# Seven products of quarters for half of an output product, in the middle of a fused attention and FFN block

## The chip, the cores and the metric

The kernel runs on one core of a Trainium2 chip. The core has five engines with queues of their own: TensorE (PE) multiplies matrices into PSUM, VectorE (DVE), ScalarE (ACT) and GpSimd (POOL) work on SBUF (and the first two on PSUM), and SyncE (SP) only issues transfers. ACT and POOL issue transfers too. Each engine takes its instructions strictly in the order of its queue. The metric is device time in microseconds (us), the median of some runs; a profiled execution gives the trace.

## The reference

Four batches of 1024 tokens with 512 channels go through an attention block and a linear FFN, both with a layer norm that is scaled and shifted per batch, and a gate:

```python
h = _layernorm(x) * (1 + ca) + sa
x = x + ga * attention(h)        # qf = h Wq^T, kf = h Wk^T; scores = 16 heads' equal q k^T
h = _layernorm(x) * (1 + cb) + sb
x = x + gb * (h @ sum_of_8_factors / sqrt(8) + bias)
```

All 16 heads have the same scores, since each head's factor is one; so the probabilities are one 1024 x 1024 matrix a batch, and V and the output projection can be folded into one matrix. Everything is float32.

## The kernel before

**The algebra.** With Wvo = Wv^T Wo^T made once, attention is softmax(q k^T) · n · W: n is the normalized x, W (`make_w`) is Wvo with the batch's scale and gate. The kernel forms Z^T = n^T · P^T first, for half of the tokens at a time (`z_steps(b, half)`), then Z · W (`attn_out`, one tile of 128 tokens at a time), divides by the softmax's denominator and adds to x. A constant row c1 is added to x (`add_c1`). Then comes the second layer norm (`ln2(b, g)`, half g), whose transposed result goes through the FFN (`ffn`, `make_f`).

**Z by quarters.** Both Z products already use Strassen's scheme: seven products m1 to m7 of quarters in place of eight, in the order m1, m5, m2, m6, m7, m3, m4 for batches 1 to 3. Their sums are taken ahead: `n_sums` on POOL (s1 to s4, L685 to L694), `p_sums` (L706, L709) and t2, t4 (L743, L779) on DVE. Each product leaves PSUM through ACT (L741, L750) or DVE (L753, L755, L761, L770, L782). L766 and L767 on POOL add two results.

**The output product.** Batches 0 to 2 use `attn_out` for all eight tiles: 4 matmuls (8 records; a float32 matmul has two) of 512 columns at L951, then L956 on DVE takes the product from PSUM, scales it by 1/denominator and adds x, and `stats` follows (L404, L406). Batch 3 uses `attn_out_quarters` for both halves: `quarter_products` makes four sums of Z (L855 to L858), `t_sums` four of W (L842 to L845), seven products of 256 columns run at L870, and DVE combines them into c (L900 to L907; ACT copies the first, L896); then L888 scales c and adds x.

**The scores.** `softmax(b, p)` does one pair of token tiles: scores on PE (L584) into one of two large PSUM tiles, maxima on DVE (L601), exponentials on ACT (L609), a reciprocal (L614), a 32 x 32 block transpose on DVE (L624), and `move_blocks` (L492): 16 transfers issued by SP, which complete the transpose. Pair 3 is done apart (`scores`, `transpose_probs`).

**Order.** While the second Z product of batch b runs (the loop over z1's seven steps k), `places` puts the projections (`project`, L538, with L552 on DVE) and the first three pairs of batch b+1 between its steps. Then come the eight `attn_out` tiles, with pair 3 and `ln2(b, 0)` in between, then the first step of batch b+1's first Z product, `ln2(b, 1)`, and in the next turn of the loop over b the rest of that Z product with `make_f`, the FFN of batch b (L1020, L1025), the bias adds (L1012) and the layer norm and transpose (`ln1`: L404, L416; `hT_by_dma`: L503) of batch b+2.

The order written in the code is a priority, not the order run: before the launch a planner fills each engine's queue by its own estimates of costs, and takes at each point the first-written instruction that it takes to be ready. `tc.keep_in_program_order` pins an instruction behind the one written before it for that engine (the c1 adds L478 have it); `follow(op, others)` pins op behind the others. Both order the queue and wait for nothing.

**Buffers.** `ps_m` has four PSUM buffers for all products. `stg` has four staging buffers (s1, s2, s4, t of one batch), `stp` two ("st": staging of transposes), `prp` two ("pr": probabilities, and c). W and f share one buffer. `ln2` of half 0 issues its 16 transfers on ACT, half 1 on SP; ACT then scales and shifts what has landed (L1002). In the sequence of the FFN, the four tiles of half 0 follow m6 of the next batch's first Z product, and half 1 follows m7.

Of the kernel before, what the change touches and what calls it, by code (L numbers as in the profile page):

```python
# [10 lines left out]
F32 = mybir.dt.float32  # L11
# [19 lines left out]
def kernel(  # L31
# [19 lines left out]
    P = 128  # L51
# [382 lines left out]
    def halves(g):  # L434
        return list(range(g * GT, (g + 1) * GT))
# [34 lines left out]
            load_xa(b + g, 1 - g)  # L470

    bc_c1, bc_ga = {}, {}

    def add_c1(b, tiles):
        if b not in bc_c1:
# [3 lines left out]

            tc.keep_in_program_order(add)  # L480

    def move_blocks(src, dst, *queues, c_outer=False):

        queues = queues or (nc.sync,)
        for i in range(NQ * NQ):
            r, c = divmod(i, NQ)
            if c_outer:  # L490
                r, c = c, r
            queues[i % len(queues)].dma_start(out=dst[ts(c, Q), r], in_=src[ts(r, Q), c])  # L492

    def hT_by_dma(b, g, *queues):

# [78 lines left out]
    def scores(b, p, later=False):  # L574


        qT, kT = qkT[b]
        if p == 0:
            rinv[b] = small.tile([P, NT], F32, tag="ri", bufs=2, name=f"ri_{b}")
        pss = []  # L580
        for i in (2 * p, 2 * p + 1):
            ps = ps_s.tile([P, T], F32, tag="sc", name=f"ps_sc_{b}_{i}")
            for h in range(2):
                nc.tensor.matmul(  # L584
                    ps[:, ts(h, 512)], qT[h * R : (h + 1) * R, ts(i, P)],
                    kT[h * R : (h + 1) * R, :], start=True, stop=True,
                )
            pss.append((i, ps))
        den = small.tile([P, 2], F32, tag="den", name=f"den_{b}_{p}")
        pr2 = prp.tile([P, 2 * T], F32, tag="pr", name=f"pr_{b}_{p}")  # L590


        if by_dma(b, 2 * p // GT):
            view = pr2.rearrange("p (c j k e) -> p k j c e", c=NQ, k=2, e=Q)
        else:
            view = pr2.rearrange("p (k j) -> p k j", k=2)
        probs[b, p] = pr2, view
        maxima = []
        for i, ps in pss:
            nm = small.tile([P, 1], F32, tag="nm", name=f"nm_{b}_{i}")  # L600
            nc.vector.tensor_reduce(nm, ps, AX.X, ALU.max, negate=True)  # L601
            maxima.append(nm)

        def numerators():
            for k, (i, ps) in enumerate(pss):
                pr = view[:, k]
                if len(pr.shape) > 2:
                    ps = ps.rearrange("p (j c e) -> p j c e", c=NQ, e=Q)
                exp = nc.scalar.activation(  # L609
                    pr, ps, AF.Exp, bias=maxima[k], scale=1.0, accum_out=den[:, k : k + 1]  # L610
                )
                if later:
                    tc.keep_in_program_order(exp)
            nc.vector.reciprocal(rinv[b][:, 2 * p : 2 * p + 2], den)  # L614

        if later:
            return numerators
        numerators()
# [171 lines left out]
    def make_w(b):  # L790
        bc = bc_ga[b] if b in bc_ga else spread("ga", b)
        if b + 1 < B:
            w = wbp.tile([P, KC, D], F32, tag="w", name=f"w_{b}")
        else:

            both = ptp.tile([P, 2, KC, D], F32, tag="pt", name=f"w_{b}")
            w, tsum["w"] = both[:, 0], sums_of(both[:, 1])
        for kc in range(KC):
            scaled = nc.vector.scalar_tensor_tensor(
                w[:, kc, :], wvo[:, kc, :], first["ca1"][:, kc, b : b + 1], bc, ALU.mult, ALU.mult  # L800
# [2 lines left out]

                tc.keep_in_program_order(scaled)
        wb[b] = w
        if b + 1 == B:
            t_sums(w, tsum["w"])

    def make_f(b):
        bc = spread("gb", b)  # L810
# [9 lines left out]
        fb[b] = f  # L820
        if b + 1 == B:
            t_sums(f, tsum["f"])

# [20 lines left out]
        tt(t3, b22, b12, ALU.subtract)  # L844
        tt(t4, b21, t2, ALU.subtract)  # L845

    def quarter_products(name, a, m, tm, engine):
# [4 lines left out]
        pr = prp.tile([P, KC, D], F32, tag="pr", name=f"sums_{name}")  # L852
        s1, s2, s3, s4 = sums_of(pr)
        tt = engine.tensor_tensor
        tt(s1, a21, a22, ALU.add)  # L855
        tt(s2, s1, a11, ALU.subtract)
# [19 lines left out]
        return product  # L876

    def attn_out_quarters(b, half):
        product = quarter_products(f"o_{b}_{half}", ZT[b, half], wb[b], tsum["w"], nc.vector)
        c = prp.tile([P, GT, D], F32, tag="pr", name=f"c_{b}_{half}")  # L880

        def cq(i, h):
# [82 lines left out]
    def ln2(b, g, ahead=None, between=None):  # L965
# [99 lines left out]
    for b in range(B):  # L1065
# [148 lines left out]
```

## Time and profile before

| | us |
|---|---|
| median of 3 runs | 518.86 (516.21 to 518.98) |
| profiled execution | 516.97 |
| its span, first to last instruction | 515.2 |
| PE busy (matmuls) | 507.4, 98% |
| DVE busy | 403.8, 78% |
| ACT busy | 91.6, 18% |
| POOL busy | 181.1, 35% |
| granted PE clock, mean | 0.999 |

PE's records are pipelined and overlap, so a record's duration (381 ns for 256 columns, 593 for 512) is longer than the distance between two. Durations of DVE overlap a little too: sums of 128 x 512 elements last 0.68 us by the record and follow each other every 0.60 us.

### The profile page before, as it was taken

Reading aid. Unit: us, or ns where it says so; the run is one execution under the profiler, and the core shown is the slowest. Engines: PE = TensorE matmul, PEld = TensorE weight load, DVE = VectorE, ACT = ScalarE, POOL = GpSimd, SP = SyncE. Lnnn points to the kernel's source line nnn. Section 1 sums busy time; section 2 is a strip of 40 time slices with the busy share of each in tenths; the row PEclk is TensorE's granted clock in tenths of the full one; section 3 lists DMA queues with packets and bytes.
Section 4 is the critical chain, followed back from the end, with each engine's and each line's share of the span. In section 5 each row is a group of like instructions: output and inputs, shape, how many; then the busy total and the mean of one; then the engine's idle time right before and its main releaser. Section 6 shows DMA issues by size and latency. Waiting matters only on the chain.

```text
span 515.2 us, 5746 instructions
## 1 busy us (share of the span) xinstructions
PE 507.4 (98%) x1888; PEld 327.5 (64%) x1888; DVE 403.8 (78%) x638; ACT 91.6 (18%) x148; POOL 181.1 (35%) x183
## 2 busy tenths in 40 slices
PE   9999999999999999999999999999999999999996
PEld 5534787664466547765457457666448488878585
DVE  4759999686999994379999994268999739889895
ACT  1327300231103200222103100122202020002020
POOL 1072324799860453630001344431001040022532
PEclk9999999999999999999999999999999999999999
DMA  8982576378654769114453657304445432003053
GB/s 311 381 309 65 136 169 194 110 241 277 184 137 109 228 199 268 38 27 102 120 135 91 182 143 254 94 0 98 117 106 129 132 107 69 0 1 102 20 174 113
DMA packets 40133, 73.06 MB, mean 142 GB/s; under 512 B 9908, under 2 KB 12468, under 8 KB 40104
## 3 DMA queue, kind: packets, MB, share of 16 engines
q1 hardware_dynamic: 27464, 40.14, 27.5%
q0 software_dynamic: 8416, 27.43, 17.0%
q10 hardware_dynamic: 4224, 5.12, 3.8%
q8 instruction: 15, 0.25, 0.2%
q14 instruction: 14, 0.11, 0.1%
HBM read 34.88 MB, written 8.42 MB: 84 GB/s over the span
## 4 chain that ended last, share of the span: by engine, by line
PE 64%; DVE 15%; SPq 6%; DMA 5%; POOL 3%; issue 3%; ACT 2%; ACTq 1%; DVEq 0%; POOLq 0%
PE ps_z_m L728 24%; PE ps_f L1020 15%; SPq L492 6%; PE ps_o L951 5%; PE ps_f_m L870 5%; PE ps_o_m L870 5%; PE ps_qk L538 4%; DMA pt<-pr 4%; PE ps_wvo L211 3%; DVE pr L624 3%; DVE nm L601 2%; ACT pr L609 1%; DVE hT_f L995 1%; ACTq L492 1%; DVE hT_f L416 1%
## 5 line engine op out<-in xcount | busy, mean ns | idle before, releaser
L728 PE MATMUL ps_z_m<-pt,xn_a 128*128 128x256 f32 x512 | 116.1, 381 | 0.4 <-DVE zt L753 0.4
L728 PEld LDWEIGHTS ps_z_m<-pt,xn_a 128*128 128x128 f32 x512 | 96.4, 190 | 22.2 <-issue 4.9
L1020 PE MATMUL ps_f<-f,hT_f 128*128 128x512 f32 x192 | 83.9, 593 | 0.4 <-ACT hT_f L1002 0.3
L951 PE MATMUL ps_o<-w,zt 128*128 128x512 f32 x192 | 83.7, 594 | 0.0
L951 PEld LDWEIGHTS ps_o<-w,zt 128*128 128x128 f32 x192 | 36.2, 190 | 45.5 <-issue 42.3
L1020 PEld LDWEIGHTS ps_f<-f,hT_f 128*128 128x128 f32 x192 | 36.3, 190 | 44.1 <-issue 39.2
L728 PE MATMUL ps_z_m<-pt,s 128*128 128x256 f32 x256 | 58.2, 380 | 0.0
L728 PEld LDWEIGHTS ps_z_m<-pt,s 128*128 128x128 f32 x256 | 48.4, 190 | 10.9 <-issue 4.7
L609 ACT ACTIVATE pr<-ps_sc,nm 128x1024 f32<-128x1024 f32 x32 | 35.5, 1113 | 88.6 <-DVE nm L601 62.0
L601 DVE TENSOR_REDUCE nm<-ps_sc 128x1 f32<-128x1024 f32 x32 | 37.6, 1210 | 3.8 <-PE ps_sc L584 3.8
L584 PE MATMUL ps_sc<-kT,qT 64*128 64x512 f32 x128 | 34.7, 622 | 1.4 <-ACT pr L609 1.4
L1002 ACT ACTIVATE hT_f<-st_f,mod_sb,mod_cb 128x512 f32<-128x512 f32 x32 | 23.4, 802 | 65.5 <-DMA st_f<-hT_f 41.8
L379 POOL TENSOR_TENSOR fsum<-fsum,factor 128x1024 f32<-128x1024 f32 x14 | 33.7, 2428 | 2.4 <-DMA factor<-in_factors_dram 2.3
L624 DVE STREAM_TRANSPOSE pr<-pr 128x2048 f32<-128x2048 f32 x14 | 32.2, 2297 | 0.5 <-issue 0.2
L741 ACT COPY zt<-ps_z_m 128x512 f32<-128x512 f32 x8 | 4.7, 587 | 153.3 <-PE ps_z_m L728 85.1
L1027 POOL DMA_DIRECT2D out_dram<-x x24 | 13.4, 560 | 49.5 <-DVE x L1025 38.4
L397 POOL TENSOR_TENSOR r_f<-v_f,mhalf 128x4 f32<-128x4 f32 x8 | 12.1, 1516 | 51.3 <-DVE v_f L391 51.2
L728 PE MATMUL ps_z_m<-t,s 128*128 128x256 f32 x128 | 29.0, 380 | 0.0
L538 PE MATMUL ps_qk<-hT_a,wqk 128*128 128x512 f32 x64 | 28.7, 593 | 0.0
L728 PEld LDWEIGHTS ps_z_m<-t,s 128*128 128x128 f32 x128 | 24.2, 190 | 5.4 <-issue 2.3
L397 POOL TENSOR_TENSOR r_a<-v_a,mhalf 128x4 f32<-128x4 f32 x8 | 10.0, 1245 | 46.5 <-DVE v_a L391 46.4
L766 POOL TENSOR_TENSOR zt<-zt 128x512 f32<-128x512 f32 x6 | 7.7, 1283 | 47.2 <-DVE mv L406 27.6
(175 smaller groups left out, 683.4 us busy)
## 6 DMA issues: line engine op xcount, KB each, us to landing
pt<-pr SPq DMA_DIRECT2D x216, 64.0 KB, 2.0
factor<-in_factors_dram POOLq DMA_DIRECT2D x7, 1024.0 KB, 6.6
out_dram<-x POOLq DMA_DIRECT2D x24, 256.0 KB, 3.0
xa<-in_x_dram POOLq DMA_DIRECT2D x20, 256.0 KB, 4.3
x<-in_x_dram POOLq DMA_DIRECT2D x20, 256.0 KB, 6.0
hT_a<-st_a SPq DMA_DIRECT2D x72, 64.0 KB, 3.7
st_f<-hT_f SPq DMA_DIRECT2D x64, 64.0 KB, 2.0
st_f<-hT_f ACTq DMA_DIRECT2D x58, 64.0 KB, 2.1
```

Source lines behind the costliest of these rows:

```text
L379: add = nc.gpsimd.tensor_tensor(part, part, f[r][:, ts(k, 2), :], ALU.add)
L492: queues[i % len(queues)].dma_start(out=dst[ts(c, Q), r], in_=src[ts(r, Q), c])
L538: nc.tensor.matmul(ps[: 2 * R, :], wqkb[b][:, kc, :], hT[:, kc] if b == 0 else hT[:, :, kc], start=(kc == 0), stop=(kc == KC - 1),)
L584: nc.tensor.matmul(ps[:, ts(h, 512)], qT[h * R : (h + 1) * R, ts(i, P)], kT[h * R : (h + 1) * R, :], start=True, stop=True,)
L601: nc.vector.tensor_reduce(nm, ps, AX.X, ALU.max, negate=True)
L609: exp = nc.scalar.activation(pr, ps, AF.Exp, bias=maxima[k], scale=1.0, accum_out=den[:, k : k + 1])
L624: nc.vector.transpose(pr2, pr2)
L728: nc.tensor.matmul(ps[:, ts(dc, 2 * P)], a[:, j, ts(dc, P)], q, start=(j == 0), stop=(j == GT - 1),)
L870: nc.tensor.matmul(ps[:, ts(i, 2 * P)], st[:, kc, ts(i, P)], mv[:, kc, :], start=(kc == 0), stop=(kc == 1),)
L951: nc.tensor.matmul(ps, ZT[b, half][:, kc, ts(j, P)], wb[b][:, kc, :], start=(kc == 0), stop=(kc == KC - 1),)
L1002: nc.scalar.activation(dst, src, AF.Identity, bias=sb, scale=cb1)
L1020: nc.tensor.matmul(ps, hT2[b, g][:, kc, ts(j, P)], fb[b][:, kc, :], start=(kc == 0), stop=(kc == KC - 1),)
```

## The change

In batches 1 and 2 (the second and third) the output product of half 0 is made by `attn_out_quarters`, as in batch 3. It stands in the loop over the second Z product, behind step 3 (m6) and ahead of the first pair of scores; the third pair moves from step 5 to step 6. `make_w` makes the four sums of W for these batches, in a tile of `stp`; the four sums of Z are put into the staging tiles s1 and t of the Z product, so they keep these from the next batch's sums until the products have read them. The c1 adds of half 0 move to step 2, those of half 1 to step 4. After the loop only tiles 4 to 7 are left for `attn_out`; pair 3 of the scores stands after tile 5, and `p_sums` ahead of tile 6. `ln2` of half 0 of batches 1 and 2 pins its transfers on ACT behind the last exponential.

```diff
-    def move_blocks(src, dst, *queues, c_outer=False):
+    def move_blocks(src, dst, *queues, c_outer=False, behind=()):
...
-            queues[i % len(queues)].dma_start(out=dst[ts(c, Q), r], in_=src[ts(r, Q), c])
+            dma = queues[i % len(queues)].dma_start(
+                out=dst[ts(c, Q), r], in_=src[ts(r, Q), c]
+            )
+            follow(dma, behind)
...
+                last_exp[:] = [exp]
...
             w = wbp.tile([P, KC, D], F32, tag="w", name=f"w_{b}")
+            if b > 0:
+                tsum["w", b] = sums_of(stp.tile([P, KC, D], F32, tag="st", name=f"w_sums_{b}"))
...
-        if b + 1 == B:
-            t_sums(w, tsum["w"])
+        if b > 0:
+            t_sums(w, tsum["w", b])
...
-        product = quarter_products(f"o_{b}_{half}", ZT[b, half], wb[b], tsum["w"], nc.vector)
+        sums = None
+        if b + 1 < B:
+
+            n1, t1 = nsum[b][0], nsum[b][4].rearrange("p r j w -> p (r j w)")
+            sums = [n1[:, ts(i, 2)] for i in range(2)]
+            sums += [
+                t1[:, ts(i, 512)].rearrange("p (k d) -> p k d", k=2) for i in range(2)
+            ]
+        product = quarter_products(
+            f"o_{b}_{half}", ZT[b, half], wb[b], tsum["w", b], nc.vector, sums
+        )
...
-        move_blocks(xn.rearrange("p (c n) -> p c n", c=NQ), st, *queues, c_outer=last)
+        move_blocks(
+            xn.rearrange("p (c n) -> p c n", c=NQ), st, *queues, c_outer=last,
+
+            behind=last_exp if g == 0 and 0 < b and not last else (),
+        )
...
-            places = (1 if b == 0 else 0, 2, 3, 4, 5)
+            places = (1, 2, 3, 4, 5) if b == 0 else (0, 2, 3, 4, 6)
...
             step()
+            if b > 0 and k == 3 and nb is not None:
+                attn_out_quarters(b, 0)
             if k in todo:
                 todo[k]()
...
-            if b > 0 and k >= 3 and nb is not None:
-                add_c1(b, range(2 * (k - 3), 2 * (k - 2)))
-            if nb is None and k == 2:
-                add_c1(b, range(NT))
+            if b > 0 and k == 2:
+                add_c1(b, halves(0) if nb is not None else range(NT))
+            if b > 0 and k == 4 and nb is not None:
+                add_c1(b, halves(1))
...
-        for t in halves(0):
+        for t in halves(0) if b == 0 else halves(1)[:2]:
             attn_out(b, t)
-            if t == 2:
+            if t % GT == (2 if b == 0 else 1):
                 scores(nb, 3)
...
-        for t in halves(1)[:2]:
-            attn_out(b, t)
-        if b > 0:
+        if b == 0:
+            for t in halves(1)[:2]:
+                attn_out(b, t)
+        else:
             p_sums(nb, 0)
```

More of the change, by code (lines that the diff above doesn't have):

```diff
@@ L472 @@
     bc_c1, bc_ga = {}, {}
+    last_exp = []
     def add_c1(b, tiles):
@@ L793, in make_w @@
             w = wbp.tile([P, KC, D], F32, tag="w", name=f"w_{b}")
+            if b > 0:
+                tsum["w", b] = sums_of(stp.tile([P, KC, D], F32, tag="st", name=f"w_sums_{b}"))
         else:
             both = ptp.tile([P, 2, KC, D], F32, tag="pt", name=f"w_{b}")
-            w, tsum["w"] = both[:, 0], sums_of(both[:, 1])
+            w, tsum["w", b] = both[:, 0], sums_of(both[:, 1])
         for kc in range(KC):
@@ L845, in t_sums, with quarter_products @@
         tt(t4, b21, t2, ALU.subtract)
-    def quarter_products(name, a, m, tm, engine):
+    def quarter_products(name, a, m, tm, engine, sums=None):
         a11, a12, a21, a22 = (quarter(a, kh, h) for h in range(2) for kh in range(2))
         b11, b12, b21, b22 = (quarter(m, kh, h) for kh in range(2) for h in range(2))
-        pr = prp.tile([P, KC, D], F32, tag="pr", name=f"sums_{name}")
-        s1, s2, s3, s4 = sums_of(pr)
+        if sums is None:
+            sums = sums_of(prp.tile([P, KC, D], F32, tag="pr", name=f"sums_{name}"))
+        s1, s2, s3, s4 = sums
         tt = engine.tensor_tensor
```

## The prediction

> **What bounds the kernel now.** I read the page's busy times first: TensorE (PE) is busy for 507.4 of 515.2 us at a granted clock of 0.999, so anything that saves matmul time looks like a gain. VectorE (DVE) is busy for 403.8 us, 78%, which is an average over stages. So next the stretches of batch index 1 (the second batch; the code's b counts from 0): columns are stretch, its length, PE, PEld, DVE, ACT, POOL busy.
>
> ```profile
> 192.20:219.90 27.70, 27.70 (x113) 21.09 (x111) 10.18 (x12) 3.90 (x6) 13.29 (x13) 1.00 0.53 143
> 219.90:237.40 17.50, 16.95 (x74) 11.04 (x74) 14.70 (x17) 4.64 (x8) 4.89 (x3) 1.00 0.22 53
> 237.40:280.80 43.40, 43.40 (x138) 24.93 (x137) 40.93 (x64) 8.61 (x14) 4.11 (x3) 1.00 0.45 113
> ```
>
> The reader is to see a cold stretch (DVE 10.2 of 27.7 us) and then a hot one: 40.9 of 43.4 us. Then the PE timeline (start, duration), where the work to be replaced stands:
>
> ```profile
> 216.37 3.62 PE L728 MATMUL ps_z_m<-pt,s 128*128 128x256 f32 x16
> 219.92 1.99 PE L584 MATMUL ps_sc<-kT,qT 64*128 64x512 f32 x8
> 221.84 3.72 PE L728 MATMUL ps_z_m<-pt,xn_a 128*128 128x256 f32 x16
> 225.49 1.99 PE L584 MATMUL ps_sc<-kT,qT 64*128 64x512 f32 x8
> ...
> 231.68 2.23 PE L584 MATMUL ps_sc<-kT,qT 64*128 64x512 f32 x8 [0.56 <-ACT pr L609]
> 233.84 3.72 PE L728 MATMUL ps_z_m<-pt,xn_a 128*128 128x256 f32 x16
> 237.39 10.46 PE L951 MATMUL ps_o<-w,zt 128*128 128x512 f32 x24
> ```
>
> Last the chain that ended last, in order of time: after 250 us it runs through DVE without a gap until one DVE instruction, L753, gives a PSUM buffer back, and only then through PE.
>
> ```profile
> 283.89 0.02 issue
> 283.92 0.02 POOLq L397
> ...
> 284.03 1.32 POOL r_a L397
> ...
> 285.97 1.32 DVE xn_a L416 x3
> 287.29 0.61 DVE zt L753
> 287.90 0.04 issue
> 287.95 7.13 PE ps_f L1020 x16
> ```
>
> The product that L753 reads (m6 of batch 2's first Z product) ended on PE at 280.79. So DVE is 6.5 us late there, and PE's third FFN tile (PE had done two, 2 x 3.43 us, by 287.65) waits 0.3 us for it. In this stretch both engines bind: PE time saved without DVE time saved is worth nothing there.
>
> **PE's part.** Four tiles of the old form are 32 records. A form with the same shape, four FFN tiles, takes 13.73 us; the seven products as batch 3 has them take 12.09 us for 56 records:
>
> ```profile
> 298.54 13.73 PE ps_f L1020 x32
> 438.72 12.09 PE ps_o_m L870 x56
> ```
>
> Saving: 1.64 us a batch, 3.3 us for two. That is the whole gain on offer, besides two waits of 0.56 us at the third pair of scores.
>
> **What is added on DVE, before the hot stretch.** Per batch: four sums of W (L842 to L845 stand 0.60 us apart in batch 3) and four of Z (L855 to L858, the same), 4.8 us. The four c1 adds of half 0 (0.60 each, 2.4) move here too; they are pinned behind the second projection's L552 (216.57), so they end at 219.7. All 7.2 us lie where DVE idles 17.5 of 27.7 us: priced at nothing, 7.2 us if that idle time were gone. The new tile for W's sums takes a staging buffer whose transfers ended by 205; the Z sums borrow s1 and t, whose last reader, m5, ends at 209.5, ten microseconds before need.
>
> **What is added at the hot stretch's start.** Batch 3 shows the same work on DVE: L900 starts 7.2 us after the first product, the last statistics end 17.3 us after it. From m6's end at 219.92 that gives DVE idle from 221.5 to 227.1, and the rows done at 237.3. Nothing fills the idle 5.6 us: the other c1 adds are pinned behind a later transpose, and the scores come after the products.
>
> [...] The sums for the next batch's Z (GpSimd, L685 to L694, 2.35 us each) ran from 209.74; now the buffers they wait for are read until 219.9 (s2), 226.8 (s1) and 230.3 (t), so the last of them falls on L888, which reads c and x from SBUF. The trace has such a meeting: L779 takes 2445 ns beside L686, and 1209 alone, so 1.2 us more. [...] I take 1.3, near the row: DVE is free at 238.6 (239.6 by the rule, and the end moves as much).
>
> **The scores.** The first pair's scores now run on PE at 232.0 to 233.9, but their maxima (L601) are written after the rows, so DVE reaches them at 238.6 instead of 221.4. Behind them wait the exponentials, the transpose, and on SP's queue 64 transfers:
>
> ```profile
> 227.50 41.70 SPq L492 DMA_DIRECT2D pt<-pr  x64
> 272.72 0.33 SPq L268 DMA_DIRECT2D bc_ga<-rows_ga  x1
> 279.48 10.02 SPq L492 DMA_DIRECT2D st_f<-hT_f  x16
> ```
>
> Maxima 2.3, exponential 1.1 after them, transpose 2.2: SP starts at 244.5 and is through at 286.2, so st_f of half 1 is issued until 296.3, 6.8 us later than now. Landing takes 2.0 us (median), the scalings L1002 begin at 298.3, and the FFN's second half can start at 299.1; before, it started at 298.4. The second pair lands at 267.3. PE finds the second pair's PSUM occupied until 240.9; m3, which is ready, can go first, or PE waits 3.5 us at 237.4. Since DVE is what binds until 290, I count neither.
>
> The new order on ACT (st_f's 16 issues of half 0, 10.2 us, behind the last exponential) costs nothing: issued from 267.3 to 277.4 against 265.2 to 275.4 now, scalings begin at 279.4, PE needs them at 280. Without that cover, each us later is a us on PE.
>
> **DVE's list from 238.6 to L753,** durations by the trace: eight maxima 9.1; four transposes and reciprocals 9.3; L761, L770, L782 1.8; c1 of half 1 2.4; tiles 4 to 7 (add, statistics) 5.4; two layer norms with transposes 8.3; L706, L709 2.4; L743 1.2; f 2.4; L779 1.2; statistics of the next but one batch 2.8 and its L416 1.9. Sum 48.2. To it come waits for exponentials and for GpSimd's powers, 2.5 us (5.6 in the old list; less here, since a fuller queue has something to do). L753 starts at 289.3 and ends at 289.9, against 287.9 now. The same sum for the old order (plus 2.4 of c1, 5.4 of tiles 0 to 3, six bias adds 3.5, waits 5.6, from 221.4) gives 286.5 where the trace has 287.3; with that error 290.7. So **+2.0 to +2.8 us for batch 1 to 2; I take +2.2.** [...] SP's transfers (299.1) then lie under the FFN's shifted second half (300.3) and cost nothing.
>
> **Batch 2 to 3** has no next but one batch: 2.8 + 1.9 + 0.9 us fall out of the list, L753 is in time (PE needs it at 287.9, counted as in batch 1). PE gains 1.64, and loses 1.9 where m5's t waits for the second pair (L706 ends at 270.6; scores' waits of 0.6 included, m5 is due at 268.7), or 0.8 if m2 goes first (those waits, and a PSUM buffer that tile 6's add gives back): −0.8 to +0.3 us, I take −0.3.
>
> **Sum: +2.2 − 0.3 = +1.9 us.** Against the profiled execution (515.2 span, 1.8 around it, 517.0): 518.9. The runs shown have a median of 518.86, 1.9 above the profiled one, so the forecast is 518.86 + 1.9 = **520.8**.
>
> **Rivals.**
> *The saving holds.* For it: PE is busy 98%, and L753 may be queued ahead of the next but one batch's L416 and its wait for GpSimd (2.8 us), where nothing needs it early. Against it: it stands behind them now, though it was ready 6.5 us before. Then L753 ends at 287 or before, PE keeps 1 to 1.6 us a batch, and the waits of 0.56 may go: 518.86 − 2.0 to − 4.4, about 515.7.
> *The bias adds stay in front of L753* (slower). Six of them (L1012, 0.59 each) stand before it now. If the planner still sees idle time there, L753 ends 3.5 us later in batch 1 to 2; in batch 2 to 3 eight (4.7 us) stand before it, of which the 3.3 us between 284.6 and 287.9 hide the most. It decides as soon as L753 ends after 287.9. Price 3.5 + 1.4, with the 1.9: 518.86 + 6.8 = 525.7. For it: the old queue. Against it: a fuller DVE leaves the planner fewer gaps to put them in.
> *The change does nothing that can be seen:* that DVE's list and PE's saving just cancel, 518.9; it is the near end of my forecast, not another mechanism.
>
> **How the numbers follow.** Likeliest case (518.4 to 522.5) 0.46, saving holds 0.26, bias adds in front 0.28. The range takes in the most of both rivals: 515.6 to 525.8, with 1 in 10 beyond each end. The likeliest case's own range is 518.4 to 522.5. About 0.5% (2.6 us; 516.3 and 521.5) is what a measurement of this kernel tells from no change. Faster: 0.22 (most of the second case). Same: 0.34 of the first and 0.04 of the second, 0.38. Slower: 0.12 and 0.28, 0.40.
>
> **What would show it.** PE: seven products in 12.1 us after m6. DVE: L900 7.2 us after the first product, the first L601 behind the statistics, near 239. POOL: L685 near 220 and not 210, L888 over 1 us. SP: the 64 transfers beginning near 244.5. L753 ending near 290, with PE's third FFN tile waiting for it. I am wrong if L601 comes ahead of the rows, if L753 ends before 288 (then the saving holds), or if PE waits for scores, t or st_f by more than 2 us.

## The result, and the profile after

The changed kernel takes **525.23 us** (median of 4 runs, 523.67 to 527.06) against 518.92 us (516.21 to 519.08) for the kernel before on the same chip: ratio 1.0135, 95% interval 1.0088 to 1.0183. It is slower by 6.3 us. The forecast was 520.8 us, in a range from 515.6 to 525.8. The kernel before runs either near 516.5 us (mean granted clock 0.998 to 1.000) or near 519 (mostly 0.995 to 0.997), and three of its four runs here were of the second sort, where the longer series below have medians of 516.8 to 518.1; so 6.3 us is rather too little than too much. The profiled execution took 524.71 us with a span of 522.9 us, 7.7 more than the span before.

In the new listing most lines have moved by 4 to 23: the Z products are L733 (were L728), the quarter products L879 (L870), the scores L588, maxima L605, exponentials L613, probabilities' transpose L629, transfers L493, the two adds of m6 L758 and L760 (L753, L755), m7's L766, m3's L775, m4's L787, `attn_out` L970 and L975, rows of the recombination L919 to L926 and L907 (L900 to L907, L888), `ln2`'s transpose L1014, scalings L1025, bias adds L1035, FFN L1043 and L1048.

First the stretches of batch index 1, with the ends of the prediction (m3's start, m6's end, 17.5 us later, and the end of the next m6; columns: stretch, length, busy time of PE, PEld, DVE, ACT, POOL, granted clock, DMA share, GB/s):

```profile
192.90:220.60 27.70, 27.70 (x114) 21.30 (x113) 16.38 (x24) 3.90 (x6) 5.33 (x10) 1.00 0.49 143
220.60:238.10 17.50, 17.50 (x81) 14.08 (x79) 11.38 (x17) 0.73 (x2) 9.43 (x4) 1.00 0.00 0
238.10:282.90 44.80, 41.76 (x155) 26.09 (x154) 43.82 (x62) 12.46 (x21) 5.51 (x5) 1.00 0.45 112
```

DVE's added work went into the cold stretch as planned (16.4 us there, 10.2 before). But in the hot stretch PE, which had been busy for the whole of 43.4 us, is now busy for 41.8 of 44.8. The PE timeline (start, duration, and in brackets the wait ahead and what ended it) shows where the 3 us stand:

```profile
220.58 3.62 PE L879 MATMUL ps_o_m<-w,zt 128*128 128x256 f32 x16
...
232.76 1.99 PE L588 MATMUL ps_sc<-kT,qT 64*128 64x512 f32 x8
234.68 3.72 PE L733 MATMUL ps_z_m<-pt,xn_a 128*128 128x256 f32 x16
239.22 1.13 PE L588 MATMUL ps_sc<-kT,qT 64*128 64x512 f32 x4 [0.82 <-ACT pr L613]
240.28 0.70 PE L733 MATMUL ps_z_m<-pt,s 128*128 128x256 f32 x2
242.86 1.13 PE L588 MATMUL ps_sc<-kT,qT 64*128 64x512 f32 x4 [1.89 <-ACT pr L613]
243.92 3.29 PE L733 MATMUL ps_z_m<-pt,s 128*128 128x256 f32 x14
```

The seven products took 12.2 us (220.58 to 232.76); this part of the saving is there. Then the second pair of scores waits twice, 2.71 us together, for the exponentials of the first pair, which must empty the PSUM tile. m3, which was ready, lies behind them in PE's queue but for 2 records. The exponentials wait for the maxima, and DVE's timeline shows why these are late:

```profile
232.06 2.75 DVE L907 SCALAR_TENSOR_TENSOR x<-c,ri,x 128x512 f32<-128x512 f32 x2
...
236.68 1.18 DVE L605 TENSOR_REDUCE nm<-ps_sc 128x1 f32<-128x1024 f32 x1
237.79 1.40 DVE L907 SCALAR_TENSOR_TENSOR x<-c,ri,x 128x512 f32<-128x512 f32 x2
...
240.39 1.18 DVE L605 TENSOR_REDUCE nm<-ps_sc 128x1 f32<-128x1024 f32 x1
```

The scores were ready at 234.7, and the rows of the recombination (L907, with their statistics) stand ahead of both maxima. Batch 2 has the same two waits (0.81 and 1.89 us at 363.01 and 366.65).

In the FFN stage the chain that ended last no longer goes from L758 to PE. L758 ends at 288.8, and PE needs its buffer at 289.75 only (282.88 and two tiles of 3.43 us). The chain runs on through DVE and POOL for another 20 us, to the add behind an FFN tile:

```profile
288.19 0.57 DVE zt L758
...
288.86 0.57 DVE x L1035
...
309.17 0.61 DVE x L1048
309.77 0.04 issue
309.82 2.41 PE ps_f L1043 x5
```

PE's waits in that stage, by its timeline:

```profile
272.42 3.72 PE L733 MATMUL ps_z_m<-t,s 128*128 128x256 f32 x16 [0.34 <-DVE t L711]
...
298.17 3.72 PE L733 MATMUL ps_z_m<-pt,xn_a 128*128 128x256 f32 x16 [1.39 <-DVE x L1048]
...
309.82 7.13 PE L1043 MATMUL ps_f<-f,hT_f 128*128 128x512 f32 x16 [0.73 <-DVE x L1048]
```

and DVE's queue ahead of the L1048 that m7 waits for:

```profile
292.53 1.89 DVE L1035 TENSOR_TENSOR x<-x,bc_gbias 128x512 f32<-128x512 f32 x3
295.61 0.69 DVE L404 BATCH_NORM_STATS2 bn_a<-xa 128x6 f32<-128x512 f32 x1 [1.20 <-DMA xa<-in_x_dram]
...
297.46 0.66 DVE L1048 TENSOR_TENSOR x<-ps_f,x 128x512 f32<-128x512 f32 x1
```

Three bias adds and a statistic that waits 1.20 us for its own transfer stand ahead of an add that gives PE a PSUM buffer.

A ledger by stage, in us from starts of products in the traces. The first column goes from m6 of the second Z product to m1 of the next batch's first one, the FFN stage from there to m3 of that product, the third column again from m6 to m1, one batch later, and "rest" from there to the end. Between the FFN stage and the third column lie 24.13 us in both kernels.

| | batch 1: m6 to m1 | FFN stage | batch 2: m6 to m1 | rest |
|---|---|---|---|---|
| before | 50.61 | 45.13 | 50.60 | 128.36 |
| after | 51.33 | 48.33 | 53.02 | 128.96 |

With 0.76 us from ahead of the change's place (m6 starts at 217.13 against 216.37; in the runs below it starts between 215.8 and 218.0, so this is scatter) it makes the 7.7 us of the spans.

The 53.02 of batch 2 are 1.7 more than batch 1's for the same waits. The stretches around the pause (columns as above) and m3's record show it:

```profile
364.00:368.00 4.00, 2.11 (x9) 0.89 (x8) 4.00 (x9) 1.94 (x3) 1.83 (x2) 1.00 0.00 0
368.00:372.00 4.00, 4.00 (x12) 3.17 (x12) 3.52 (x4) 1.67 (x4) 1.69 (x2) 0.57 0.13 33
```

The granted clock falls to 0.57 behind the two waits: 14 records of m3 took 4.98 us at 367.71, and 3.29 us in batch 1.

### The profile page after: what moved, and what is told of

The parts are those of the page before. It is cut to its first block, busy times and chain, and to the rows that moved or that the text cites. A ratio compares the mean times of both kernels' runs of the same rounds, so it can differ in the third digit from the quotient of the medians.

```text
span 522.9 us, 5892 instructions
## 1 busy us (share of the span) xinstructions
PE 508.2 (97%) x1936; PEld 337.4 (65%) x1936; DVE 419.6 (80%) x668; ACT 93.1 (18%) x150; POOL 175.5 (34%) x183
## 4 chain that ended last, share of the span: by engine, by line
PE 56%; DVE 19%; SPq 7%; issue 6%; DMA 6%; POOL 4%; ACTq 1%; ACT 1%; DVEq 0%; POOLq 0%
PE ps_z_m L733 24%; PE ps_f L1043 10%; PE ps_o_m L879 7%; SPq L493 7%; PE ps_qk L542 4%; DMA pt<-pr 4%; PE ps_wvo L211 3%; PE ps_o L970 3%; DVE pr L629 2%; DVE nm L605 2%; DVE bn_f L404 2%; DMA st_f<-hT_f 2%; DVE x L907 2%; PE ps_f_m L879 1%; ACTq L493 1%
## 5 line engine op out<-in xcount | busy, mean ns | idle before, releaser
L733 PE MATMUL ps_z_m<-pt,xn_a 128*128 128x256 f32 x512 | 116.0, 381 | 1.8 <-DVE x L1048 1.4
L733 PEld LDWEIGHTS ps_z_m<-pt,xn_a 128*128 128x128 f32 x512 | 96.5, 190 | 22.6 <-issue 3.4
L1043 PE MATMUL ps_f<-f,hT_f 128*128 128x512 f32 x192 | 84.1, 594 | 1.3 <-DVE x L1048 0.7
L1043 PEld LDWEIGHTS ps_f<-f,hT_f 128*128 128x128 f32 x192 | 36.1, 190 | 45.4 <-issue 37.3
L733 PE MATMUL ps_z_m<-pt,s 128*128 128x256 f32 x256 | 60.4, 389 | 0.0
L733 PEld LDWEIGHTS ps_z_m<-pt,s 128*128 128x128 f32 x256 | 49.4, 194 | 12.8 <-issue 6.2
L970 PE MATMUL ps_o<-w,zt 128*128 128x512 f32 x128 | 56.4, 596 | 0.0
L613 ACT ACTIVATE pr<-ps_sc,nm 128x1024 f32<-128x1024 f32 x32 | 35.5, 1113 | 114.1 <-DVE nm L605 60.9
L970 PEld LDWEIGHTS ps_o<-w,zt 128*128 128x128 f32 x128 | 23.9, 190 | 31.6 <-issue 30.5
L605 DVE TENSOR_REDUCE nm<-ps_sc 128x1 f32<-128x1024 f32 x32 | 37.9, 1202 | 3.8 <-PE ps_sc L588 3.8
L588 PE MATMUL ps_sc<-kT,qT 64*128 64x512 f32 x128 | 34.8, 622 | 5.7 <-ACT pr L613 5.7
L1025 ACT ACTIVATE hT_f<-st_f,mod_sb,mod_cb 128x512 f32<-128x512 f32 x32 | 23.4, 803 | 72.1 <-DMA st_f<-hT_f 47.6
L629 DVE STREAM_TRANSPOSE pr<-pr 128x2048 f32<-128x2048 f32 x14 | 32.1, 2290 | 0.2 <-DMA pt<-pr 0.2
L733 PE MATMUL ps_z_m<-t,s 128*128 128x256 f32 x128 | 29.2, 381 | 0.3 <-DVE t L711 0.3
L733 PEld LDWEIGHTS ps_z_m<-t,s 128*128 128x128 f32 x128 | 24.1, 190 | 6.4 <-issue 2.3
L397 POOL TENSOR_TENSOR r_f<-v_f,mhalf 128x4 f32<-128x4 f32 x8 | 9.9, 1237 | 49.6 <-DVE v_f L391 49.4
L588 PEld LDWEIGHTS ps_sc<-kT,qT 64*128 64x128 f32 x128 | 11.3, 185 | 22.5 <-issue 11.0
L397 POOL TENSOR_TENSOR r_a<-v_a,mhalf 128x4 f32<-128x4 f32 x8 | 8.9, 1112 | 47.3 <-DVE v_a L391 47.3
```

The costliest lines, as they stand in the source:

```text
L588: nc.tensor.matmul(ps[:, ts(h, 512)], qT[h * R : (h + 1) * R, ts(i, P)], kT[h * R : (h + 1) * R, :], start=True, stop=True,)
L613: exp = nc.scalar.activation(pr, ps, AF.Exp, bias=maxima[k], scale=1.0, accum_out=den[:, k : k + 1])
L629: nc.vector.transpose(pr2, pr2)
L733: nc.tensor.matmul(ps[:, ts(dc, 2 * P)], a[:, j, ts(dc, P)], q, start=(j == 0), stop=(j == GT - 1),)
L970: nc.tensor.matmul(ps, ZT[b, half][:, kc, ts(j, P)], wb[b][:, kc, :], start=(kc == 0), stop=(kc == KC - 1),)
L1025: nc.scalar.activation(dst, src, AF.Identity, bias=sb, scale=cb1)
```

## The experiments

Theory A: what the change loses is PE's wait for a DVE queue in which the late scores stand behind the rows, and the saving was real. Rivals, named in each expectation: the late transfers behind the scores, and DVE's sum of work, which no order would mend. Theory B in an expectation is whichever of the two rivals that run is to tell apart from A; experiment 6 has Q and T instead, for DVE's order and the late transfers of the FFN stage. The labels in brackets are those that the expectations use. All kernels of this section compute the whole result. In the order of the runs; the first four share one chip, where the kernel before had a median of 517.43.

**1. Scores ahead of the products** (`e1_scores_first`). Two statements change places; the rest of the change stays.

```diff
+            if k in todo:
+                todo[k]()
             if b > 0 and k == 3 and nb is not None:
                 attn_out_quarters(b, 0)
-            if k in todo:
-                todo[k]()
```

> The changed kernel with the first pair of scores put ahead of the seven products instead of behind them. Theory A (DVE's queue: the recombination, c's scaling and the statistics stand ahead of the first pair's maxima, so PSUM for the second pair comes free late and DVE idles 5.5 us before the first recombination): maxima near 222 in place of 236.7 and 240.5, the two waits of 0.8 and 1.9 us at the second pair's scores fall under 0.5, the granted clock stays at 1.00 near 366 us, PE's waits of 1.4 and 0.7 us in the FFN shrink: 516 to 518.5 us, at or under the kernel before. Theory B (SP's 64 transfers, begun 18 us later, cost the time): only the first 16 of them begin earlier, the other 48 stay where they are: 523 to 525 us.

Measured: 518.15 us (12 runs), ratio to before 1.0010 (0.9985 to 1.0034). The waits at the second pair are gone, and with them most of the FFN stage's (45.23 us; batches 50.49 and 50.51). Theory A's number held. (It leaves open how much of the FFN stage's gain is DVE's order there: with the earlier scores the transfers of half 1's st_f start at 282.1 as well, and not at 288.3.) Yet PE's saving of 1.64 us a batch still does not show, for a new wait takes its place. PE's timeline of this kernel, and DVE's:

```profile
252.37 5.42 PE L970 MATMUL ps_o<-w,zt 128*128 128x512 f32 x12 [2.13 <-DVE zt L787]
```

```profile
228.86 0.69 DVE L919 TENSOR_TENSOR c<-ps_o_m,c 128x512 f32<-128x512 f32 x1 [1.70 <-PE ps_o_m L879]
...
248.66 2.46 DVE L479 TENSOR_TENSOR x<-x,bc_c 128x512 f32<-128x512 f32 x4
251.04 0.68 DVE L775 TENSOR_TENSOR zt<-ps_z_m,zt 128x512 f32<-128x512 f32 x1
251.64 0.68 DVE L787 TENSOR_TENSOR zt<-ps_z_m,zt 128x512 f32<-128x512 f32 x1
```

The c1 adds of half 1 (2.46 us) stand ahead of m4's add, whose input PE had finished by 246.4. The wait of 2.15 us in batch 2 is the same.

**2. The place alone** (`e2_moved_only`). The four tiles of the old form at the place of the products, no sums, no products; the scores behind, as in the change.

```diff
...
-                attn_out_quarters(b, 0)
+                for t in halves(0):
+                    attn_out(b, t)
```

> The changed kernel with everything moved as in it, but tiles 0 to 3 made by the old form (four matmuls of 512 columns a tile) at the place of the seven products, without the sums of W and Z. PE has 1.65 us more work a batch than the changed kernel. Theory A: DVE takes each tile as it comes and is done about 2 us after PE's last one, so the maxima are late by 2 us at most, the waits at the second pair are under 1 us: 519 to 521.5 us. If the place alone (scores 12 us later) costs the time, as in theory B, it is 523 us or more.

Measured: 519.52 us, ratio 1.0034 (1.0018 to 1.0050); m6 to m1 51.54 and 51.69 us, with a wait of 1.38 us for L787 in each batch, and the FFN stage 46.01, with one of 1.01 us for a scaling. Theory A's number held here too. The old form takes each tile out of PSUM as it is done, while PE goes on with the next, so that DVE is nearly through when the scores come: there is no wait at the second pair, though the first pair stands at the same place. The place costs 2 us, with PE's work as in the kernel before. The other 4 of the change's 6.3 come with the products, although they save PE 3.3: their recombination begins only 7.2 us after the first product starts, and its rows are done only after the scores have come.

**3. Rows later** (`e3_rows_later`). The change, with the rows (L907 and statistics) written behind the first pair.

```diff
-        rows(0)
+        if later is None:
+            rows(0)
         tt(cq(1, 0), product(4), cq(1, 0), ALU.add)
-        rows(1)
+        if later is None:
+            rows(1)
+        else:
+            later.extend([lambda: rows(0), lambda: rows(1)])
...
+            for step in later:
+                step()
```

> The changed kernel with c's scaling and the statistics (about 5.5 us of DVE work) written behind the first pair's transpose instead of ahead of its maxima; products and recombination stay. Theory A: first maxima near 234 to 236, no wait at the second pair's first tile, but the moved work stands in front of the second pair's maxima, so some of the wait moves to the third pair: 520 to 523.5 us. Theory B: SP begins about 4 us earlier of 18: 523.5 to 525 us.

Measured: 523.64 us, ratio 1.0110 (1.0075 to 1.0145). The total is just outside theory A's 520 to 523.5 and just inside theory B's 523.5 to 525, so it decides nothing by itself. The trace does: the second pair waits 0.60 us instead of 2.71, but now PE waits 2.98 and 3.00 us for L787, and the clock falls behind both pauses (a mean of 0.54 from 255 to 258 us, and of 0.76 from 376 to 380). The same 12 records of `attn_out` that take 5.42 us in the first experiment take 6.99 and 7.02 here:

```profile
255.44 6.99 PE L974 MATMUL ps_o<-w,zt 128*128 128x512 f32 x12 [2.98 <-DVE zt L787]
```

The stage costs 53.94 and 53.99 us, the FFN stage 44.74. The wait moved with the rows, and grew.

**4. Two queues** (`e4_two_queues`). The change, with the transfers of the first two pairs split over SP and POOL.

```diff
-            work += [lambda p=p: softmax(nb, p) for p in range(len(places) - 2)]
+            two = (nc.sync, nc.gpsimd) if b > 0 else ()
+            work += [
+                lambda p=p: softmax(nb, p, *(two if p < 2 else ()))
+                for p in range(len(places) - 2)
+            ]
```

> The changed kernel with the first two pairs' 32 transfers issued by SP and POOL in turn, so that each pair is issued in about 5.2 us instead of 10.4 and the 64 are through about 10 us sooner. Theory A: the waits at the second pair's scores (2.7 us a batch) come before any of these transfers and stay: 523.5 to 526 us, unless POOL's powers are held up. Theory B: the late transfers are what costs: 520 to 522.5 us.

Measured: 520.08 us, ratio 1.0056 (1.0033 to 1.0080). The waits at the second pair are as in the change (0.81 and 1.89, twice), so the transfers do not cause them. But the total is what theory B expected (520 to 522.5), not A's 523.5 to 526, for the FFN stage falls from 48.33 to 44.85: st_f of half 1 is issued from 284.0 instead of 288.3. So the waits at the second pair are not the whole loss; nearly half of it lies in the FFN stage. The planner changed DVE's order as well here (the first two L1048 at 293.6 and 296.0, the second ahead of the statistics), so the run doesn't say which of the two did it.

**5. The c1 adds in the gap** (`e5_c1_in_gap`). The first experiment, and the c1 adds of half 1 moved into DVE's idle 1.70 us ahead of L919 (the diff is against the first experiment).

```diff
             if b > 0 and k == 3 and nb is not None:
+                add_c1(b, halves(1))
                 attn_out_quarters(b, 0)
...
-            if b > 0 and k == 4 and nb is not None:
-                add_c1(b, halves(1))
```

> Scores first, as in e1_scores_first, and the four c1 adds of half 1 moved from behind the quarter products to ahead of them, so that VectorE does them in the 1.7 us in which it stood idle before the first recombination. The whole result is computed. Theory A (what TensorE waits for in the changed kernel is VectorE's queue behind the late scores; with the scores first, what is left is the c1 adds, 2.46 us ahead of the adds L775 and L787): the wait of 2.13 us for L787 in attn_out's tile 5 is gone in both batches, start of m6 to start of m1 is 48.4 us in both instead of 50.5 (e1) and 50.6 (before), total 4 us below e1 and below before: 513 to 514.5 in a job where before is at 517.5. Theory B (VectorE binds over the whole stretch up to L758 and its sum of work counts, not its order at one place): the saving of 4.2 us comes back as later waits in the FFN stage (m1 to m3 45.2 us in e1, 47 or more here), total 516.5 to 518.5, the same as before.

Measured: 524.96 us (6 runs), ratio 1.0146 (1.0109 to 1.0182); neither theory gave that (513 to 514.5, and 516.5 to 518.5). DVE's timeline of this kernel, with POOL's line in the second fence, shows two things:

```profile
250.18 0.68 DVE L1035 TENSOR_TENSOR x<-x,bc_gbias 128x512 f32<-128x512 f32 x1
250.78 2.30 DVE L1014 STREAM_TRANSPOSE hT_f<-hT_f 128x2048 f32<-128x2048 f32 x1
253.01 0.65 DVE L787 TENSOR_TENSOR zt<-ps_z_m,zt 128x512 f32<-128x512 f32 x1
...
349.84 4.64 DVE L479 TENSOR_TENSOR x<-x,bc_c 128x512 f32<-128x512 f32 x4
```

```profile
351.59 2.34 POOL L698 TENSOR_TENSOR s<-s,xn_a 128x1024 f32<-128x1024 f32 x1 [4.23 <-PE ps_o_m L879]
```

The planner filled the room that the c1 adds left with a bias add and a transpose, so that L787 came at 253.0 and PE waited 2.99 and 3.00 us. And in batch 2 the four adds met a POOL sum and took 4.64 us instead of 2.46; the products waited 1.90 us for L919. A drop of the granted clock behind the wait of 3.00 us adds 1.7 in batch 2 (a mean of 0.54 from 378 to 380 us; 12 records of `attn_out` took 7.09 us; stage 55.21 us). L758, too, came late now, by 1.79 us: that is the wait that the prediction had named.

**6. Statistics behind** (`e6_stats_behind`). The change, with the waiting statistics pinned behind the second L1048 (`ffn_second` holds that add).

```diff
...
-            stats(xa[b, t], mv1[b], t, f"a_{b}_{t}", m6_second if (b, g) == (2, 0) else ())
+            stats(xa[b, t], mv1[b], t, f"a_{b}_{t}", {(2, 0): m6_second, (3, 1): ffn_second}.get((b, g), ()))
```

> The changed kernel, with the statistics of the next but one batch's tiles 2 and 3 (L404 bn_a 4 to 7) pinned behind the FFN's second bias-free add (L1048 of tile 1), so that no wait for the transfer of xa stands ahead of L1048. Only the step from batch 1 to 2 is touched. The whole result is computed. Theory Q (m7's wait of 1.39 us and tile 6's of 0.73 in batch 1's FFN stage come from VectorE's queue order: bias adds and a waiting statistic ahead of L1048): m7 no longer waits, m1 to m3 falls from 48.3 us to 45.5 to 46.5, total 2 to 2.5 us below the changed kernel, about 522.5 to 523.2 where that is 525.2. Theory T (the late transfers to st_f's half 1 hold the stage; L1048 merely follows): m1 to m3 stays at 48 us or more, total 525, and the wait is put down to the scaling L1025 or to the transfers instead.

Measured: 525.72 us, ratio 1.0159 (1.0125 to 1.0193). The local claim of theory Q is borne out: m7 no longer waits, and the stage falls to 46.45 us, inside the 45.5 to 46.5; its number for the total (522.5 to 523.2) failed. What lies right behind is theory T's wait, by PE's timeline:

```profile
301.77 14.00 PE L1043 MATMUL ps_f<-f,hT_f 128*128 128x512 f32 x32 [1.24 <-ACT hT_f L1025]
```

The transfers of st_f for half 1 are issued until 298.3 here, and this scaling starts at 300.9. The total did not fall. In the profiled execution the clock dropped in batch 1 too (a mean of 0.67 from 244 to 248 us; its m3 took 4.98 us; stage 53.03, that is 1.70 more than in the change), which nearly cancels the FFN stage's gain of 1.88.

**7. Without the new order on ACT** (`e7_no_behind`). `behind=()` in place of the pin behind the last exponential.

> The changed kernel without its new order on ScalarE (st_f's 16 transfers of half 0 pinned behind the last exponential): the planner puts 1 of them ahead of the third pair's exponential and 13 ahead of the fourth's, and VectorE's queue has L1048 further ahead. The whole result is computed. Prediction's step (the order costs nothing, since the scalings need st_f only at 280): if the pin does nothing for better or worse, 525.2 as the changed kernel. If the pin was needed: the fourth pair's exponential starts some 8 us later (13 issues of 0.64 us), the fourth pair's transpose on VectorE and the transfers of half 1's second pair with it; PE waits for t (L711) or zt before m5, and the total is 527 to 531. If the pin cost something through VectorE's order behind it: L1048 comes sooner, m7 waits less, 522.5 to 524.

Measured: 526.2 us, ratio 1.0152 (1.0120 to 1.0185), 1.0 above the changed kernel, which was not measured beside it and has an interval that overlaps. As expected, 9 issues of st_f (5.78 us) stand directly ahead of the fourth pair's exponential, and one ahead of the third pair's; PE waits 1.28 us for the latter (0.89 in batch 2) and 2.25 for a scaling L1025, while m7's wait for L1048 is gone. The total lies between the answers, so no loss or gain can be told; that the pin cost nothing, as the prediction had it, fits, for nothing was gained without it.

**8. DVE's queue by hand** (`e10_m4_first`). The scores first, as in 1, and at L787 the order pinned: transpose L1014 and bias adds L1035 behind m4's add (kept in `m4_done`), the c1 adds of half 1 behind it too. The diff is against the first experiment.

```diff
...
-            nc.vector.transpose(xn, xn)
+            follow(nc.vector.transpose(xn, xn), m4_done if 0 < b and g == 0 else ())
...
-            if b == 0:
-                follow(add, m6_second)
+            follow(add, m4_done if b > 0 else m6_second)
...
-            if b > 0 and k == 4 and nb is not None:
+            if b > 0 and k == 6 and nb is not None:
                 add_c1(b, halves(1))
```

> Scores first, as in e1_scores_first, and VectorE's queue ordered by hand where TensorE waits: the feature transpose L1014 of half 0 and the bias adds (L1035) pinned behind m4's add (L787), the c1 adds of half 1 moved behind it too. The whole result is computed. Theory A (order of VectorE's queue at L787 is what TensorE pays for): L787 ends near 250.4 instead of 252.3, so attn_out's tile 5 waits 0.2 us or nothing instead of 2.13 in both batches, start of m6 to start of m1 falls from 50.5 (e1) to 48.5, and the FFN stage stays near 45.2 (L760 now stands ahead of the next statistics' L416): 514 to 515 where before is at 518. Theory B (VectorE's sum of work binds, the order only shifts where it shows): what is won at L787 comes back at the next instruction of the queue, the c1 adds ahead of the L975s of tiles 4 and 5 or L758, by 2 us or more a batch, 517 to 519.

Measured: 516.94 us, where the kernel before had 516.79 on the same chip: ratio 0.9999 (0.9983 to 1.0015). The wait for L787 is 0.20 us, and m6 to m1 is 48.56 and 48.57 us, as theory A has it. But the FFN stage is at 46.79 and the rest at 130.99, with PE waiting 0.66 and 1.28 us for scalings L1025 and 0.37 for L758. So the total is theory B's, no better than before: what was gained at L787 came back later, as B has it.

**9. The c1 adds earlier** (`e12_c1_early`). As 8, but the adds of half 1 ahead of the second projection, where DVE idles 1.9 and 1.6 us: now they leave the hot stretch for good. The diff is against experiment 8.

```diff
+            if b > 0 and k == 1 and nb is not None:
+                add_c1(b, halves(1))
...
-            if b > 0 and k == 6 and nb is not None:
-                add_c1(b, halves(1))
```

> As e10_m4_first, but the c1 adds of half 1 stand ahead of the second projection (L556 of the second half), where VectorE idles 1.9 and 1.6 us. The whole result is computed. Theory A: no wait for L787 and 2.4 us of work taken out of VectorE's hot stretch for good: start of m6 to start of m1 48.4 us in both batches (e1 50.5, before 50.6), the FFN stage 44.7 to 45.3 us (before 45.1): 513.5 to 515 where before is at 518, faster than both kernels. Theory B (sum of work): the saving shows in the FFN stage too only as far as the 2.4 us go, so 515 to 516.5. [...]

Measured: 514.11 us (11 runs), ratio to before 0.9941 (0.9916 to 0.9966), faster than both kernels; m6 to m1 48.55 and 48.58 us as theory A has it, the FFN stage 46.63, which is over A's 44.7 to 45.3. The kernel before stood at 516.79 here and not at the 518 of the expectation; 2.7 us below it is in theory B's range (1.5 to 3), not in A's (3 to 4.5).

**10. The control, and 9 again** (`e13_before_pins`, `e12_again`). Is that the seven products, or the order, which might have helped the kernel before too? The control has the old form, with the pins and the places of the c1 adds of 9; both ran on one chip.

> Control: the kernel before, without the seven products, with the same hand-made order on VectorE as e12_c1_early (L1014's and L1035's counterparts pinned behind m4's add, c1 adds of half 1 ahead of the second projection, those of half 0 behind it). The whole result is computed. If the gain of e12 is the seven products (1.64 us a batch on TensorE) laid bare by the order: start of m6 to start of m1 is 50.2 us in both batches here (48.55 in e12, plus 1.64), the total 0 to 1 us below before, 516 to 517, and 2.5 to 3.5 above e12. If it is the order alone, which would have helped the kernel before as well: 513.5 to 514.5, as e12.

> e12_c1_early once more, beside its control on the same chip: 513.5 to 514.7, 2.2 to 3.2 us below before, if the gain of 0.59% is real; the waits of its first profile (L787 0.2 us, L758 0.67, L1025 0.70) again.

Measured, with the kernel before at 517.94: the control 515.35 us (17 runs), ratio 0.9962 (0.9942 to 0.9982); 9 again 514.71 us (12 runs), ratio 0.9944 (0.9920 to 0.9967). Neither answer of the control was right: the order by itself brings 2.6 us. In the control PE has no wait above 0.1 us between 205 us and the end, where the kernel before had two of 0.56; m6 to m1 is 49.74 us in both batches, the FFN stage 45.09. By PE's timeline of the control:

```profile
216.26 3.62 PE L728 MATMUL ps_z_m<-pt,s 128*128 128x256 f32 x16
...
266.00 3.62 PE L728 MATMUL ps_z_m<-pt,xn_a 128*128 128x256 f32 x16
```

With the products it is 48.54 and 48.55, so 1.2 of the forecast 1.64 us a batch are really saved, and the waits ahead of the FFN tiles give back most of it (FFN stage 45.80, rest 129.1 against 128.4), by PE's timeline of 9 again:

```profile
251.08 5.42 PE L970 MATMUL ps_o<-w,zt 128*128 128x512 f32 x12 [0.19 <-DVE zt L787]
286.81 7.13 PE L1042 MATMUL ps_f<-f,hT_f 128*128 128x512 f32 x16 [0.66 <-DVE zt L758]
369.56 5.42 PE L970 MATMUL ps_o<-w,zt 128*128 128x512 f32 x12 [0.19 <-DVE zt L787]
398.28 14.00 PE L1042 MATMUL ps_f<-f,hT_f 128*128 128x512 f32 x32 [0.51 <-ACT hT_f L1025]
```

What the seven products bring on top of a good order is 0.64 us by the medians, and the two intervals overlap: it can't be told from nothing. DVE's sum of work, the rival that no order would mend, is thus not refuted: with the best order found, what DVE was given on top took most of PE's saving back.

## Why the prediction was wrong

It forecast no change that can be told, with a lean to slower; the kernel is slower by 6.3 us. The time lies in the range, near its upper end, and close to the rival "the bias adds stay in front of L753" (525.7), but not by that rival's mechanism.

**What held.** PE's part: 12.2 us for the products against 12.09 forecast. DVE idle ahead of the first recombination, which starts 7.2 us after the first product (227.76). GpSimd's sums pushed to 220.8 and later, with one falling on the rows, at a price of 1.35 us where 1.3 was taken. (The 239.6 that the prediction sets beside its 238.6 takes 2.35 us, a whole sum, in place of the 1.3. No run shows a rule for it: the row in the change shows 1.35, a c1 add in experiment 5 2.2.) SP's 64 transfers start at 245.79 (forecast 244.5), and half 1's follow:

```profile
245.79 42.37 SPq L493 DMA_DIRECT2D pt<-pr  x64
288.26 10.29 SPq L493 DMA_DIRECT2D st_f<-hT_f  x16
```

The free order on ACT cost nothing that can be told (experiment 7). L758 ended at 288.8, 1.1 before the forecast, but with some luck. The six bias adds were all to fall behind it; four of the eight (L1035) still stood ahead of it, 2.4 us, as in this line of DVE's timeline:

```profile
256.69 0.68 DVE L1035 TENSOR_TENSOR x<-x,bc_gbias 128x512 f32<-128x512 f32 x1
```

Against that the L416 of the next but one batch (1.9 us) stood behind it, and DVE idled 1.0 us on the way where 2.5 us of waits were taken.

**The step that failed** is in the part on the scores: "PE finds the second pair's PSUM occupied until 240.9; m3, which is ready, can go first, or PE waits 3.5 us at 237.4. Since DVE is what binds until 290, I count neither." PE waited 2.71 us in batch 1 and 2.70 in batch 2, and behind the second the clock fell (0.50 from 368.2 to 371.6 us).

In **batch 2 to 3** nothing covers these waits, by the prediction's own account: L753 is in time there. Yet its sum has 0.6 us for them, and nothing for the clock. Here the forecast was −0.3 and the ledger has +3.0: 2.4 in the stage, of which 1.7 are the granted clock, and 0.6 in the rest (by PE's starts 0.2 up to the FFN stage and 0.4 in the last FFN of the kernel).

In **batch 1 to 2** the step was sound on its own terms. PE would have reached the third FFN tile at about 286.0 (287.65 − 1.64), L753 was to end at 289.9, and a wait of 3.5 us would have been hidden behind it. But PE's waits came first, and L758 was no longer what PE waited for. From m6 to that tile PE needed 72.6 us where it had needed 71.6: 1.0 more, less than the 2.2 forecast. Each wait costs some 0.3 us more than its length, an estimate from the trace: records overlap by 0.17 us in an unbroken stream, and the first product after a wait is slower (m5 took 3.56 us and m7 3.66 to the next start, 3.45 undisturbed). So the stage from m6 to m1 costs −1.64 (products) − 0.86 (the old wait at the third pair, 0.56) + 3.3 (the two new ones): +0.8, where the ledger has +0.72. With the scores first (experiment 1) these waits go, and with them 6 to 7 us in all, the FFN stage's included.

**The second failing step** is that what stands behind L753 costs nothing, the bias adds above all. One stood just behind L758, and three more stood ahead of L1048, which holds a PSUM buffer as L753 does. The prediction looked at one instruction by which DVE gives PE a buffer and not at the next one. Price: the waits of 1.39 and 0.73 for L1048 and 0.34 for t make 2.46, with three restarts 3.4, less the old 0.3: 3.1 of the FFN stage's +3.2. Experiment 6 shows DVE's order as the first layer of it (−1.9 us) and the late transfers of st_f as a second (1.24 us) that the first had hidden; the prediction had these transfers cost nothing under an FFN that L753 had shifted. How experiment 4's 3.5 us divide between the two stays open.

So batch 1 to 2 cost 3.9 us by the ledger (forecast +2.2): less than forecast up to the third FFN tile, and nearly all the rest behind it. That the total came near the rival of the bias adds is chance. Four of them did stand in front of L758, but PE never waited for it.

## What to carry to other kernels

Where two engines are both near full, every place at which the one hands the other a buffer or an operand is a deadline of its own: go through all of them in the order of the queue, and set a wait found early at nothing only where the lateness that is to hide it is sure to come. Here it did not. An improvement measured together with a reordering needs a control with the reordering alone: here the order was worth 2.6 us, and the products with all their added VectorE work 0.6, which can't be told from nothing.

## What the runs showed of the hardware

**In these profiles the granted clock fell for 3.4 us at a time, behind waits of 2.7 to 3 us, and not every time.** The pair of waits of 0.8 and 1.9 us within 5 us stands at eight places of the profiled executions (the change, experiments 4, 6 and 7), and a single one of 3.0 at four (3 and 5); the clock fell at five of the eight and at three of the four. At the eleven places with a single wait of 1.2 to 2.3 us it did not. Where it fell it cost the same: 12 records took 6.99, 7.02 and 7.09 us instead of 5.42, 14 records 4.98 instead of 3.29, so 1.6 to 1.7 us. How long it was down shows in the change, in a narrower stretch than the 4 us from 368 (columns as above):

```profile
368.20:371.60 3.40, 3.40 (x9) 2.68 (x9) 3.32 (x4) 1.22 (x3) 1.49 (x2) 0.50 0.15 36
```

The 0.2 us ahead of it have 1.00 and the 0.4 behind it 0.98. At six of the other seven places the means of the stretches around the drop (0.54 from 255 to 258 us and 0.92 from 258 to 262 in experiment 3, for one) come to 3.4 or 3.5 us, an estimate that takes 0.50 for the clock there too.

What condition brings a drop about is not shown. Between the two waits of the pair PE worked for 1.8 us, the single waits were 3.0, and the clock fell behind both. Nor did every drop stand behind such a wait. In experiment 4 the clock was at 0.50 at 27 us too (its mean over that execution is 0.991, that of the change 0.996), behind a stretch of short matmuls with no wait above 0.28 us since the first one, where the kernel before and the change have 1.00:

```profile
27.00:30.00 3.00, 3.00 (x4) 1.17 (x4) 0.73 (x4) 0.00 (x0) 2.12 (x2) 0.50 1.05 386
```

What brings that one about stays open too.

**VectorE beside GpSimd.** Two VectorE instructions that met a GpSimd sum under way ended 0.55 us after it. The first two lines are from the change, the two below from experiment 5; alone the two VectorE instructions take 0.74 and 0.68 us:

```profile
232.06 2.09 DVE L907 SCALAR_TENSOR_TENSOR x<-c,ri,x 128x512 f32<-128x512 f32 x1
231.25 2.35 POOL L699 TENSOR_TENSOR s<-xn_a,s 128x1024 f32<-128x1024 f32 x1 [1.15 <-PE ps_o_m L879]
```

```profile
351.61 2.87 DVE L479 TENSOR_TENSOR x<-x,bc_c 128x512 f32<-128x512 f32 x1
351.59 2.34 POOL L698 TENSOR_TENSOR s<-s,xn_a 128x1024 f32<-128x1024 f32 x1 [4.23 <-PE ps_o_m L879]
```

In these two the price was 0.1 to 0.2 us less than what was left of the GpSimd instruction: 1.35 us for L907, which came 0.81 us into it (1.54 left), and 2.2 for the c1 add, which began 0.02 us into it (2.32 left). Elsewhere it was the GpSimd sum that took longer. In the kernel before, L693 began at 214.46 us, while L779 ran on until 215.58, and took 3.33 us; the sums ahead of it and behind it (L685, L686, L694) took 2.34 to 2.35. The forecast's 1.3, taken from one meeting of another pair, was right by luck of timing; the 2.2 us of experiment 5 were as possible.
